# Six of 25 source-alpha lookups of a GAT layer as gathers from a table in DRAM, with residual steps moved

## Chip, cores, metric

One core of one Trainium2 chip runs the whole kernel. The metric is device time in microseconds of one launch, median of the runs shown.

## What is computed

Two graph attention layers over N = 3125 nodes and E = 53125 edges (sorted by destination, a self loop for each node in the list and one more added in each layer), on x of 3125 x 768, added to x:

```python
h = jnp.maximum(_layernorm(x), 0.0)
# one layer: xl = (h @ W).reshape(n, heads, out_ch)
alpha_src = jnp.einsum('nhc,hc->nh', xl, a_src)
alpha_dst = jnp.einsum('nhc,hc->nh', xl, a_dst)
e = jax.nn.leaky_relu(alpha_src[src] + alpha_dst[dst], 0.2)
m = jax.ops.segment_max(e, dst, num_segments=n)
e = jnp.exp(e - m[dst])
s = jax.ops.segment_sum(e, dst, num_segments=n)
alpha = e / (s[dst] + 1e-16)
out = jax.ops.segment_sum(xl[src] * alpha[:, :, None], dst, num_segments=n)
```

Layer 1 has 4 heads of 256 channels (joined to 1024), layer 2 one head of 768. After each layer come a layer norm and a residual product: layer 1 adds h @ Wr1 + br1 after a ReLU, layer 2 h1 @ Wr2 + br2. The change concerns `alpha_src[src]` of layer 1.

## The kernel before

The nodes are cut into NB = 25 tiles of 128 destinations (the last has 53). The edges of a tile stand in J = 17 slots of 128 each (fewer in the last), so one tile has 2176 slots. For each slot `idx_s` holds the source node, `rel_s` the destination within the tile.

The program runs in this order.

1. **Products.** For each tile x is normalised and multiplied by W1; eight more columns give the source and destination alphas of the 4 heads. The rows go to `table1` in DRAM (L218 stores them on SP), the alphas to `asad1` in SBUF (L876, ACT). Beside this the slot lists are made, and the destination alphas of all slots (`own`). 80 KB of one-hot per tile go to DRAM from POOL (L939).
2. **Residual tiles.** The residual h0 @ Wr1 of the twelve tiles kept in SBUF is a generator, `early()`: 24 residual tiles, each of six matmuls of 128 x 512 (L1008, f32, two records each in the profile), after which ACT adds the bias out of PSUM (L1011) and SP stores the result (L1015). It yields after every matmul: one yield is one step, 144 in all. The PSUM tile `pm` has three buffers. Steps are handed out between other work of TensorE (`next(fill, None)`).
3. **Lookups of source alphas** (loop at L1083). For each of the 25 tiles SP loads the list of source nodes modulo 128, 544 KB (L1087, tile `s`), DVE makes a one-hot of it (L530, `ohs`) and one of the source's tile number (L1090, `ohh`); TensorE multiplies the one-hot by all alphas, 51 matmuls into four PSUM tiles `pq` (L562); DVE picks the right tile's column (four L564) and reduces to `al1[:, :, :, b]` (L567). Ahead of each lookup stand 4 or 5 steps.
4. **Weights** (L1101, function `weights`). 17 transposes turn the alphas into rows (L581), DVE runs a maximum over each destination in both directions (L627, L628), 17 transposes turn it back (L592), DVE and ACT make the exponentials. The argument `(5, 13, 8)` gives the steps ahead of, between and behind the transposes.
5. **Sums of layer 1.** For each tile the rows of `table1` are gathered by POOL, 128 rows of 4 KB at a time, into 16 buffers (L197, L201), and TensorE adds them up by weight (L757), tile by tile in five rounds. `pace` gives for each tile and round how many steps of the late tiles' residual (`later()`, two matmuls per step, L182) stand behind the round. In the first rounds of the first tile `first()` also makes the totals: transposes (L581), a scan (L648), transposes back (L592).
6. **Layer 2**: products, gathers and sums of the second table, and the output.

The order on TensorE is the order of the code. In stages 2 and 3 ACT, DVE, POOL and SP are ordered by a scheduler from dependences and its own estimates; each engine then runs its list in that order, and an instruction that waits holds up those behind it.

Of the kernel before, what the change touches and what calls it, by code (L numbers as in the profile page):

```python
# [10 lines left out]
F32 = mybir.dt.float32  # L11
# [5 lines left out]
AF = mybir.ActivationFunctionType  # L17
# [13 lines left out]
J = 17  # L31
# [7 lines left out]
POS = [FROM[j % 4] + j // 4 for j in range(J)]  # L39
# [29 lines left out]
def in_order(  # L69
# [16 lines left out]
    nc = tc.nc  # L86
    N, D = x.shape
    E = src.shape[0]
    H, C1 = a_src1.shape
    HC = H * C1  # L90
    C2 = W2.shape[1]
    P = 128
    NB = -(-N // P)
# [32 lines left out]
    dram = ctx.enter_context(tc.tile_pool(name="dram", bufs=1, space=DRAM))  # L126
# [9 lines left out]
    src16_d = dram.tile([NB * S], I16, name="src16_d")  # L136
    slo16_d = dram.tile([NB * S], I16, name="slo16_d")
    keep_d = dram.tile([H * NB, S + 2], BF16, name="keep_d")
    hot_d = dram.tile([NB, 128, WIN], F8, name="hot_d")
    ball_d = dram.tile([C2], F32, name="ball_d")  # L140

# [17 lines left out]
    idx_s = const.tile([128, NB * J], I32, name="idx_s")  # L159
# [10 lines left out]
    asad1 = const.tile([P, NB, 2 * H], F32, name="asad1")  # L170
# [45 lines left out]
    def store_rows(q, dst_, b, t):  # L216
        for o, e in pieces(b):
            q.dma_start(dst_[b * P + o:b * P + e, :], t[o:e])  # L218
# [379 lines left out]
    def weights(heads, own, al, alo, keep, sr, xs, pp, nq, fill, steps):  # L598

        R = heads * NB  # L600

        def fl(t):
            return t.rearrange("p j h b -> p (j h b)")

        def leaky(t):
            nc.vector.scalar_tensor_tensor(fl(t), fl(t), SLOPE, fl(t), op0=OP.mult, op1=OP.max)  # L606

        def filled(n):
            for _ in range(n):
                next(fill, None)  # L610

        eo = sr.tile([128, J, heads, NB], F32, name="eo")
        m = sr.tile([128, J, heads, NB], F32, name="m")
        pen = sr.tile([R, S + 2], BF16, name="pen")
        fw = sr.tile([R, S], F32, name="fw")
        bw = sr.tile([R, S], F32, name="bw")
        nc.vector.tensor_scalar(pen, keep, -1.0, BIG, op0=OP.add, op1=OP.mult)
        a_s, a_d = own[:, :, :heads, :], own[:, :, heads:, :]
        to_rows, to_slots = rows_and_slots(heads, pp, "pq", nq)

        filled(steps[0])
        for _ in to_rows(al, xs):
            pass
        filled(steps[1])
        nc.vector.tensor_add(eo, a_s, a_d)
        leaky(eo)
        nc.vector.tensor_tensor_scan(fw, pen[:, 0:S], xs, 0.0, op0=OP.add, op1=OP.max)  # L627
        nc.vector.tensor_tensor_scan(bw[:, ::-1], pen[:, 1:S + 1][:, ::-1], fw[:, ::-1], 0.0,  # L628
                                     op0=OP.add, op1=OP.max)
        nc.vector.tensor_add(al, al, a_d)  # L630
        leaky(al)
        for _ in to_slots(bw, lambda js, p: nc.vector.tensor_max(m[:, js], p, a_s[:, js])):
            pass
        filled(steps[2])
        nc.vector.tensor_add(m, m, a_d)
        leaky(m)
        nc.vector.tensor_sub(al, al, m)
        nc.scalar.activation(al, al, AF.Exp)
        nc.vector.tensor_sub(eo, eo, m)
        nc.scalar.activation(alo[:, :, :heads, :], eo, AF.Exp)  # L640
# [133 lines left out]
    with tc.tile_pool(name="m1", bufs=1) as mp:  # L774
# [8 lines left out]
        with tc.tile_pool(name="h0", bufs=1) as hp, tc.tile_pool(name="pm1", bufs=1, space=PSUM) as pm1, \  # L783
# [9 lines left out]
            with tc.tile_pool(name="w1", bufs=1) as wp, tc.tile_pool(name="d1", bufs=2) as dp, \  # L793
# [60 lines left out]
                def product(b, i):  # L854

                    nonlocal known
                    r = rows_of(b)
                    if i == 0:
                        rows1[b] = wp.tile([P, HC], F32, name="row", bufs=LEAD)[:r]
                    row = rows1[b]  # L860
                    pm = pm1.tile([128, 512], F32, name="pm", bufs=3)
                    parts = 1 if r == P else 2
                    n = C // parts
                    for k in range(NK1):
                        for h in range(parts):
                            o = i * C + h * n
                            dense(pm[:, :n], h0[b][:, k, :], w1[:, k, o:o + n], r,
                                  start=(k == 0), stop=(k == NK1 - 1), at=half_at(b, h).start)
                        if k == NK1 - 1:
                            for h in range(parts):  # L870
                                o = i * C + h * n
                                e = min(o + n, HC) - o
                                at = half_at(b, h)
                                nc.scalar.activation(row[:, o:o + e], pm[at, :e], AF.Copy)
                                if e < n:
                                    nc.scalar.activation(asad1[:r, b, :], pm[at, e:n], AF.Copy)  # L876
                            if i == 2:
                                known = b + 1
                                store_rows(nc.sync, table1, b, row)
                        if k % 3 == 2:  # L880
                            yield
# [148 lines left out]
            with tc.tile_pool(name="pq1", bufs=1, space=PSUM) as pp:  # L1030
                with tc.tile_pool(name="sb1", bufs=1) as sb:
# [3 lines left out]
                    def ends_of_lists():  # L1035
# [40 lines left out]
                        yield  # L1076
                        yield from last_slots(sb, upto)

                    nc.sync.dma_start(keep1, keep_d)
                    by_chunk(g1, None, NK2, g1_c)  # L1080
                    by_chunk(be1, None, NK2, be1_c)
                    slots = ends_of_lists()
                    for b in range(NB):  # L1083
                        for _ in range(4 + b % 2):
                            next(fill, None)
                        t = sb.tile([128, S], I16, name="s", bufs=2)
                        nc.sync.dma_start(t, slo16_d[b * S:(b + 1) * S][None, :].to_broadcast([128, S]))  # L1087
                        ohs = one_hot(sb, t, S, "ohs")
                        ohh = sb.tile([128, J, NB], BF16, name="ohh", bufs=3)
                        nc.vector.tensor_tensor(  # L1090
                            ohh, iota_f[:, None, :NB].to_broadcast([128, J, NB]),
                            hi_s[:, b * J:(b + 1) * J, None].to_broadcast([128, J, NB]), OP.is_equal)
                        source_values(H, al1, b, pp, 4, group_of(H), ohs, tabs, ohh, pick)
                        next(slots, None)
                    for _ in slots:
                        pass
                    none = sb.tile([128, NB * J], F32, name="none")
                    nc.vector.tensor_scalar(none, rel_s, 0.0, float(CODE), op0=OP.is_lt, op1=OP.mult)
                    nc.vector.tensor_tensor(idx_k, none, idx_s, OP.add)
                with tc.tile_pool(name="sr1", bufs=1) as sr:  # L1100
                    weights(H, own, al1, alo1, keep1, sr, xs1, pp, 4, fill, (5, 13, 8))  # L1101
                for _ in fill:
                    pass

# [1 line left out]
        with tc.tile_pool(name="w2", bufs=1, reuse_waits="tile") as wp, tc.tile_pool(name="e1", bufs=2, reuse_waits="tile") as ep, \  # L1106
# [53 lines left out]
            def end1(b, z, share):  # L1160
# [50 lines left out]
                for i, (pm, (o, n)) in enumerate(zip(pms, halves)):  # L1211
# [4 lines left out]
                store_rows(nc.sync, table2, b, row)  # L1216

            places = [*range(2, 13), 0, 1, 13, 14, 15]
            pace = [(0, 0, 4, 5, 5), (4, 4, 3, 2, 2), (2.2, 3.4, 0, 0, 1), (3, 0, 0, 0.5, 3), (0, 0, 0.8, 3.4, 0),
                    (0, 0.8, 2.2, 3.4, 0)]  # L1220
            sums(H, C1, table1, al1, alo1_d, places, 3, gp, ap, pp, end1, more, pace, first())

# [756 lines left out]
```

## Time and profile before

| | |
|---|---|
| time, median of 3 runs | 1751.04 us (1750.64 to 1751.28) |
| profiled execution | 1749.32 us, span 1747.4 us |
| TensorE busy | 1635.8 us, 94% of the span |
| DVE / POOL / ACT busy | 1000.0 / 883.6 / 461.4 us |
| chain that ended last | TensorE 68%, DMA 18%, DVE 5% |
| granted TensorE clock, mean | 0.979 |

PE is TensorE's matmuls, PEld its weight loads, DVE VectorE, ACT ScalarE, POOL GpSimd, SP the engine that issues most plain DMAs. A timeline row gives start, duration, engine, line, operation, output and inputs, the count of records merged, and in brackets the idle time ahead of it and what ended that. A group's row gives busy time, mean ns of one, idle time ahead and its releasers. Matmuls of one row overlap a little, so a piece of work is best priced from start to start.

### The profile page before, as it was taken

The numbers are of one execution on the slowest core, as the hardware profiler recorded it, in microseconds if no ns is written. First come the engines' busy times: TensorE is split into PE (matmuls) and PEld (weight loads), VectorE is DVE, ScalarE is ACT, GpSimd is POOL, SyncE is SP. The second block draws the span as 40 slices with busy tenths as digits, with TensorE's granted clock in tenths as the row PEclk, the third lists the DMA queues.
The fourth block names the chain that finished last, engine by engine and source line by source line (L and its number), as shares of the span: only waits on it lengthen the run. The fifth ranks groups of instructions, "written<-read, shape, count | busy, mean of one in ns | idle before, by whom it ended". The sixth has DMA issues, their size and how long they took to land.

```text
span 1747.4 us, 31393 instructions
## 1 busy us (share of the span) xinstructions
PE 1635.8 (94%) x11519; PEld 929.9 (53%) x11519; DVE 1000.0 (57%) x2592; ACT 461.4 (26%) x1312; POOL 883.6 (51%) x924
## 2 busy tenths in 40 slices
PE   7999999899989999999999999987898999998994
PEld 5666666566646556556565555543444444444431
DVE  7783342798884666565565656751344544454555
ACT  2122332000122122122122121122344443434443
POOL 2000111200055766666666666736677777777773
PEclk9999999999999999999999999998999999999997
DMA  7824545743179999999999999979999999999994
GB/s 239 276 98 137 153 123 171 277 129 115 50 273 381 405 398 398 373 399 379 393 392 373 370 374 372 399 276 329 377 381 384 387 390 383 376 372 392 381 357 161
DMA packets 189924, 541.31 MB, mean 310 GB/s; under 512 B 34824, under 2 KB 83336, under 8 KB 189634
## 3 DMA queue, kind: packets, MB, share of 16 engines
q0 software_dynamic: 100912, 381.56, 57.6%
q1 hardware_dynamic: 84456, 147.27, 24.3%
q10 hardware_dynamic: 4394, 10.39, 1.5%
q8 instruction: 94, 1.54, 0.4%
q14 instruction: 68, 0.56, 0.1%
HBM read 498.62 MB, written 65.62 MB: 323 GB/s over the span
## 4 chain that ended last, share of the span: by engine, by line
PE 68%; DMA 18%; DVE 5%; issue 3%; POOL 3%; ACT 2%; POOLq 0%; SPq 0%; DVEq 0%; ACTq 0%
PE p L182 13%; DMA g<-table,idx_s 13%; PE pr L182 13%; PE pm L182 12%; PE pa L757 11%; PE pm L1008 7%; PE pa L1406 4%; PE pq L562 3%; DMA g<-table,hi_s 3%; POOL g L197 2%; PE mix L1365 1%; PE p L1182 1%; DMA w<-in_L_gnn_W_dram 1%; DMA s<-slo_d 1%; PE pt L840 1%
## 5 line engine op out<-in xcount | busy, mean ns | idle before, releaser
L197 POOL DMA_INDIRECT g<-table,idx_s x409 | 392.4, 959 | 334.9 <-DVE al L606 170.5
L201 POOL DMA_INDIRECT g<-table,hi_s x423 | 431.9, 1021 | 205.9 <-PE pa L757 88.8
L182 PE MATMUL pr<-wr,h 128*128 128x384 f32 x768 | 277.0, 507 | 3.3 <-issue 2.1
L182 PE MATMUL p<-w,h1T 128*128 128x384 f32 (+1 forms) x768 | 267.7, 496 | 0.0
L757 PE MATMUL pa<-g,w 128*32 128x256 f32 x3912 | 245.0, 384 | 9.4 <-DMA g<-table,hi_s 4.7
L182 PEld LDWEIGHTS pr<-wr,h 128*128 128x128 f32 x768 | 143.0, 196 | 112.7 <-issue 36.5
L182 PEld LDWEIGHTS p<-w,h1T 128*128 128x128 f32 x768 | 139.9, 189 | 112.9 <-issue 21.4
L757 PEld LDWEIGHTS pa<-g,w 128*32 128x32 f32 x3912 | 119.6, 110 | 128.5 <-issue 23.6
L1406 PE MATMUL pa<-g,w 128*32 128x384 f32 x1956 | 182.9, 504 | 2.6 <-DVE v L1440 2.6
L734 DVE TENSOR_TENSOR w<-oh,al 128x128 f32<-128x128 f32 (+1 forms) x416 | 132.3, 318 | 51.6 <-PE pa L757 26.8
L182 PE MATMUL pr<-h0k,wr 128*128 128x256 f32 (+1 forms) x576 | 142.2, 394 | 0.1
L1008 PE MATMUL pm<-h0g,wr 128*128 128x512 f32 x288 | 132.0, 606 | 0.0
L182 PE MATMUL pm<-w,h0l 128*128 128x344 f32 x432 | 131.9, 460 | 0.0
L182 PE MATMUL pm<-w,h0g 128*128 128x344 f32 x432 | 130.8, 459 | 0.3 <-ACT h0g L842 0.3
L939 POOL DMA_DIRECT2D hot_d<-ohd x25 | 13.4, 537 | 216.1 <-DVE own L513 122.0
L182 PEld LDWEIGHTS pr<-h0k,wr 128*128 128x128 f32 x576 | 106.5, 191 | 29.6 <-issue 10.3
L1406 PEld LDWEIGHTS pa<-g,w 128*32 128x32 f32 x1956 | 55.7, 112 | 118.1 <-issue 100.8
L733 DVE TENSOR_SCALAR oh<-iota_f,rel_s 128x32 f32<-128x32 f32 (+1 forms) x416 | 112.0, 269 | 2.0 <-issue 1.9
L182 PEld LDWEIGHTS pm<-w,h0g 128*128 128x128 f32 x432 | 81.9, 193 | 40.6 <-issue 1.6
L182 PEld LDWEIGHTS pm<-w,h0l 128*128 128x128 f32 x432 | 81.2, 192 | 39.3 <-issue 1.6
L1347 ACT ACTIVATE slots<-g 128x32 f32<-128x32 f32 x416 | 65.7, 219 | 121.2 <-DMA g<-table,idx_s 113.8
L1215 DVE COPY asad<-p 128x2 f32<-128x2 f32 (+1 forms) x25 | 4.0, 160 | 154.3 <-ACT row L1213 154.3
(302 smaller groups left out, 1702.5 us busy)
## 6 DMA issues: line engine op xcount, KB each, us to landing
s<-slo_d SPq DMA_DIRECT2D x25, 544.0 KB
table<-row SPq DMA_DIRECT2D x24, 512.0 KB
own<-table SPq DMA_DIRECT2D x24, 512.0 KB
h1T_d<-h1T SPq DMA_DIRECT2D x24, 512.0 KB
h<-h1T_d SPq DMA_DIRECT2D x88, 128.0 KB
table<-row SPq DMA_DIRECT2D x24, 392.0 KB
ring<-in_x_dram SPq DMA_DIRECT2D x24, 384.0 KB
out_dram<-z ACTq DMA_DIRECT2D x24, 384.0 KB
```

What stands on the lines that cost most here:

```text
L182: nc.tensor.matmul(out_, lhsT, rhs, start=start, stop=stop)
L197: nc.gpsimd.indirect_dma_start(out=g, out_offset=None, in_=table[:, :], in_offset=bass.IndirectOffsetOnAxis(ap=idx_s[:, c], axis=0))
L201: nc.gpsimd.indirect_dma_start(out=g, out_offset=None, in_=table[:, :], in_offset=bass.IndirectOffsetOnAxis(ap=idx_k[:, c], axis=0), bound ...
L562: nc.tensor.matmul(q[:, j], oh[:P, o:o + 128], tabs[:, i], start=(i == 0), stop=(i == 2))
L733: nc.vector.tensor_scalar(oh, iota_f[:, lo:hi], rel_s[:, c:c + 1], None, op0=OP.is_equal)
L734: nc.vector.tensor_tensor(w, oh[:, None, :].to_broadcast([128, heads, hi - lo]), al[:, POS[j], :, b:b + 1].to_broadcast([128, heads, hi - ...
L757: nc.tensor.matmul(pa[p0:p0 + 32, o // f, o % f:o % f + n], w[:, o // cols, :], g[:, o:o + n], start=to not in opened, stop=False, skip_gr ...
L840: nc.tensor.transpose(pt[:, k, :r], xt[:, (k0 + k) * 128:(k0 + k + 1) * 128], ident[:r, :r])
L1008: nc.tensor.matmul(pm, wr1[:, k, m * 128:(m + 1) * 128], groups[gi][:, k, :], start=(k == 0), stop=(k == NK1 - 1))
L1182: nc.tensor.transpose(pt[:, k, :r], z[:, (k0 + k) * 128:(k0 + k + 1) * 128], ident[:r, :r])
L1347: nc.scalar.activation(slots[b % 2][:, POS[j], :], gs[b, j][:, C2:C2 + 1].to_broadcast([128, 32]), AF.Copy)
L1406: nc.tensor.matmul(pa[p0:p0 + 32, i, :f], w_, g[:, i * f:(i + 1) * f], start=(i, q) not in opened, stop=False, skip_group_check=True)
```

## The change

The alphas of each tile are also stored as rows of a table `asrc_d` (3125 x 4 floats) in DRAM, 25 small DMAs on SP. Tiles 18 to 23 are no longer looked up: POOL gathers their alphas from that table, 17 gathers per tile of 128 rows of 16 bytes, and after the loop ACT copies each tile's result into `al1`. The other 19 tiles are looked up as before, with 102 steps spread over them and five more ahead of the first. The third argument of `weights` goes from 8 to 13, and `pace` of the first tile moves steps from its later rounds to its second.

```diff
+    asrc_d = dram.tile([N, H], F32, name="asrc_d")
...
                             if i == 2:
                                 known = b + 1
+                                nc.sync.dma_start(asrc_d[b * P:b * P + r], asad1[:r, b, :H])
                                 store_rows(nc.sync, table1, b, row)
...
+                    BY_GATHER, BESIDE = 6, 102
...
-                    for b in range(NB):
-                        for _ in range(4 + b % 2):
+                    by_gather = range(NB - 1 - BY_GATHER, NB - 1)
+                    read = {}
+                    for b in by_gather:
+                        read[b] = sb.tile([128, J, H], F32, name=f"read{b}")
+                        for j in range(J):
+                            c = b * J + j
+                            nc.gpsimd.indirect_dma_start(
+                                out=read[b][:, POS[j]], out_offset=None, in_=asrc_d[:, :],
+                                in_offset=bass.IndirectOffsetOnAxis(ap=idx_s[:, c:c + 1], axis=0))
+                    by_table = [b for b in range(NB) if b not in by_gather]
+                    for i, b in enumerate(by_table):
+                        for _ in range((i + 1) * BESIDE // len(by_table) - i * BESIDE // len(by_table) + (0 if i else 5)):
                             next(fill, None)
...
                     for _ in slots:
                         pass
+                    for b in by_gather:
+                        nc.scalar.activation(al1[:, :, :, b], read[b], AF.Copy)
...
-                    weights(H, own, al1, alo1, keep1, sr, xs1, pp, 4, fill, (5, 13, 8))
+                    weights(H, own, al1, alo1, keep1, sr, xs1, pp, 4, fill, (5, 13, 13))
...
-            pace = [(0, 0, 4, 5, 5), (4, 4, 3, 2, 2), (2.2, 3.4, 0, 0, 1), (3, 0, 0, 0.5, 3), (0, 0, 0.8, 3.4, 0),
+            pace = [(0, 3, 3, 4, 4), (4, 4, 3, 2, 2), (2.2, 3.4, 0, 0, 1), (3, 0, 0, 0.5, 3), (0, 0, 0.8, 3.4, 0),
```

How it moves instructions is shown at three places. Lines of the changed kernel are one to fifteen higher than before: L1011 becomes L1013, L197 L198, L757 L758.

ACT, from the last product on, before (`rt<-pm` is the activation behind a residual tile, `junk,cnt` a count over a one-hot, `scr<-pq` the copies behind the first 17 transposes of the weights):

```order
L876 ACTIVATE asad_108<-pm 53x8
L1011 ACTIVATE rt<-pm,br_c 128x4x128
L942 ACTIVATE junk,cnt<-ohd 128x640
L1011 ACTIVATE rt<-pm,br_c 128x4x128 x19
L583 ACTIVATE scr<-pq 100x512 x4
```

And at the same place in the changed kernel, where `al_117<-read` is the copy of one gathered tile:

```order
L1013 ACTIVATE rt<-pm,br_c 128x4x128
L1111 ACTIVATE al_117<-read_2366 128x68
L1013 ACTIVATE rt<-pm,br_c 128x4x128
L1111 ACTIVATE al_117<-read_2384 128x68
L1013 ACTIVATE rt<-pm,br_c 128x4x128
L1111 ACTIVATE al_117<-read_2402 128x68
L1013 ACTIVATE rt<-pm,br_c 128x4x128
L1111 ACTIVATE al_117<-read_2420 128x68
L1013 ACTIVATE rt<-pm,br_c 128x4x128
L1111 ACTIVATE al_117<-read_2438 128x68
L1013 ACTIVATE rt<-pm,br_c 128x4x128
L1111 ACTIVATE al_117<-read_2456 128x68
```

The first row there is the second residual activation; the six copies stand one ahead of each of the third to the eighth, not behind the loop as in the code.

POOL, behind the stores of one-hots, before (`g` is a buffer of the sums' gathers):

```order
L368 DMA w_in<-views_d,view 100x704
L939 DMA hot_d<-ohd 128x640 x25
L197 DMA g_4418<-table_64,idx_s 128x1024
L197 DMA g_4419<-table_64,idx_s 128x1024
L197 DMA g_4420<-table_64,idx_s 128x1024
```

And in the changed kernel:

```order
L941 DMA hot_d<-ohd 128x640 x25
L1092 DMA read_2366<-asrc_d,idx_s 128x4 x17
L1092 DMA read_2384<-asrc_d,idx_s 128x4 x17
L1092 DMA read_2402<-asrc_d,idx_s 128x4 x17
L1092 DMA read_2420<-asrc_d,idx_s 128x4 x17
L1092 DMA read_2438<-asrc_d,idx_s 128x4 x17
L1092 DMA read_2456<-asrc_d,idx_s 128x4 x17
L198 DMA g_4162<-table_64,idx_s 128x1024
```

All 102 small gathers go ahead of the first 4 KB gather.

TensorE, behind the last lookup, before (`pm` are residual steps, `pq<-ident` transposes, `pa` the first sum):

```order
L1008 MATMUL pm<-h0g_1348,wr_2272 128x512 x5
L581 MATMUL pq<-ident,al_116 100x128 x17
L1008 MATMUL pm<-h0g_1348,wr_2272 128x512 x13
L592 MATMUL pq<-ident,bw 128x100 x17
L1008 MATMUL pm<-h0g_1348,wr_2272 128x512 x8
L757 MATMUL pa<-g_4418,w_4435 32x256
```

And in the changed kernel:

```order
L1010 MATMUL pm<-h0g_1364,wr_2298 128x512 x5
L582 MATMUL pq<-ident,al_117 100x128 x17
L1010 MATMUL pm<-h0g_1364,wr_2298 128x512 x13
L593 MATMUL pq<-ident,bw 128x100 x17
L1010 MATMUL pm<-h0g_1364,wr_2298 128x512 x13
L758 MATMUL pa<-g_4162,w_4179 32x256
```

Five more steps stand ahead of the first sum. Two rounds of sums later, before (the transposes of the totals, then the third round):

```order
L581 MATMUL p_4536<-ident,al_116 100x128 x4
L581 MATMUL p_4542<-ident,al_116 100x128 x4
L581 MATMUL p_4548<-ident,al_116 100x128
L757 MATMUL pa<-g_4426,w_4522 32x256 x2
L757 MATMUL pa<-g_4427,w_4527 32x256
```

And in the changed kernel (`pr<-h0k` are the matmuls of the late tiles' residual):

```order
L582 MATMUL p_4280<-ident,al_117 100x128 x4
L582 MATMUL p_4286<-ident,al_117 100x128 x4
L582 MATMUL p_4292<-ident,al_117 100x128
L183 MATMUL pr<-h0k,wr_2298 128x256 x6
L758 MATMUL pa<-g_4170,w_4266 32x256 x2
```

Three steps (six matmuls), which stood in later rounds, now stand behind the totals' transposes.

## Prediction

> **What bounds the kernel now.** I read the page first, then the busy time by stage, then the timelines of PE, ACT, POOL and DVE in the stretch that the change rewrites. Three rows of the windows answer give that stretch; the columns are the window, its length, busy time of PE, PEld, DVE, ACT and POOL, then the granted clock, DMA share and GB/s.
>
> ```profile
> PE 1635.8 (94%) x11519; PEld 929.9 (53%) x11519; DVE 1000.0 (57%) x2592; ACT 461.4 (26%) x1312; POOL 883.6 (51%) x924
> 304.66:472.60 167.94, 162.91 (x1528) 102.92 (x1527) 140.48 (x226) 14.46 (x22) 10.87 (x11) 0.99 0.43 148
> 472.60:499.70 27.10, 22.14 (x79) 11.13 (x77) 26.45 (x17) 8.27 (x12) 7.58 (x5) 1.00 0.34 106
> 499.70:566.00 66.30, 60.60 (x524) 41.19 (x524) 33.32 (x107) 14.25 (x36) 38.78 (x35) 0.95 1.00 382
> ```
>
> PE sets the end nearly everywhere. In the lookup stage (304.66 to 472.60) it is busy 162.91 of 167.94 us, while POOL works 10.87. So whatever leaves PE there is a gain, unless PE is made to wait. PE's timeline prices both kinds of its work:
>
> ```profile
> 456.22 4.52 PE L1008 MATMUL pm<-h0g,wr 128*128 128x512 f32 x10
> 460.58 2.45 PE L562 MATMUL pq<-tabs,ohs 128*128 128x100 bf16 x51
> 462.86 3.66 PE L1008 MATMUL pm<-h0g,wr 128*128 128x512 f32 x8
> 466.36 2.45 PE L562 MATMUL pq<-tabs,ohs 128*128 128x100 bf16 x51
> 468.65 4.52 PE L1008 MATMUL pm<-h0g,wr 128*128 128x512 f32 x10
> 473.00 2.02 PE L581 MATMUL pq<-ident,al 128*100 128x128 f32 x17
> 474.86 11.32 PE L1008 MATMUL pm<-h0g,wr 128*128 128x512 f32 x26
> 487.11 1.65 PE L592 MATMUL pq<-ident,bw 100*128 100x100 f32 x17 [0.93 <-issue]
> 488.60 7.06 PE L1008 MATMUL pm<-h0g,wr 128*128 128x512 f32 x16
> 499.69 4.71 PE L757 MATMUL pa<-g,w 128*32 128x256 f32 x32 [4.04 <-DVE w L734]
> ```
>
> From start to start, one lookup takes 2.28 us (460.58 to 462.86) and a residual step (two L1008 records) 0.873 us (462.86 to 466.36 is four). After the lookups come the 17 transposes at 473.00, 13 steps, 17 transposes, 8 steps and a wait of 4.04 us before the sums begin at 499.69.
>
> **The change, part by part.** *Lookups removed.* Six times 2.28 is 13.7 us off PE, and five steps (4.4 us) move into the 4.04 us wait. If nothing waited, the 112 steps left after the first six, and 19 lookups, would follow from 306.48 on:
>
> ```profile
> 306.48 3.67 PE L1008 MATMUL pm<-h0g,wr 128*128 128x512 f32 x8
> 329.21 0.19 PE L1052 MATMUL pq<-mine_f,cnt 128*25 128x4 f32 x2 [4.35 <-DVE scr L564]
> 329.33 6.26 PE L1008 MATMUL pm<-h0g,wr 128*128 128x512 f32 x10
> ```
>
> 306.48 + 112 x 0.873 + 19 x 2.28 + 0.5 (three small matmul pairs) = 448.1, against 473.00 now: 24.9 us less. The early wait of 4.35 us (DVE was late) goes too in that count.
>
> *Gathers added.* 102 gathers of 16-byte rows stand first on POOL, ahead of the 4 KB gathers for the sums. None of that size is in the trace, so these rows bound it:
>
> ```profile
> L197 POOL DMA_INDIRECT g<-table,idx_s x409 | 392.4, 959 | 334.9 <-DVE al L606 170.5
> L699 POOL DMA_INDIRECT ao<-alo_d,at_last x25 | 24.7, 987 | 16.5 <-DMA alo_d<-scr 9.2 <-DVE aw L687 1.8 <-DVE oh L733 1.8
> 304.66 1.01 POOL L197 DMA_INDIRECT g<-table,idx_s  x1 [2.68 <-PE pm L1008]
> 308.49 1.21 POOL L197 DMA_INDIRECT g<-table,idx_s  x1 [0.30 <-issue]
> 313.87 0.94 POOL L197 DMA_INDIRECT g<-table,idx_s  x1 [0.30 <-issue]
> 317.60 0.98 POOL L197 DMA_INDIRECT g<-table,idx_s  x1 [0.30 <-issue]
> ```
>
> POOL's time per gather does not follow the bytes: 959 ns with rows of 3 to 4 KB, 987 with 800-byte rows (L699). What is common to them is 128 rows, as here. With the 0.30 us between them a gather costs 1.26 us; the ends are 1.24 (0.94 + 0.30) and 1.29 (304.66 to 317.60, ten gathers). So 17 gathers, one tile, take 21.4 us, and all six tiles 128.5. Begun at 304.9 (304.66 plus one more small store ahead on SP), the last leaves POOL at 433.1.
>
> *The copies added, and what queues behind them.* This decides. A tile's copy into al1 (L1111 of the changed kernel) waits for its 17 gathers and stands on ACT between the activations that empty PE's residual tiles (L1011, now L1013): the n-th copy ahead of activation n+2, as the order shows. A residual tile pm is six steps, and has three buffers, so tile n+5 cannot start on PE before activation n+2. PE runs in its written order; when it stops there, the lookups behind it stop as well.
>
> ```profile
> L1011 ACT ACTIVATE rt<-pm,br_c 128x512 f32<-128x512 f32 x24 | 16.5, 687 | 174.0 <-PE pm L1008 165.3 <-DMA s<-slo_d 6.9 <-issue 1.8
> L876 ACT ACTIVATE asad<-pm 128x8 f32<-128x8 f32 (+1 forms) x25 | 4.3, 172 | 0.0
> 124.60 0.97 SPq L410 DMA_DIRECT2D tails<-w_in  x1
> 126.89 0.35 DVE L412 SCALAR_TENSOR_TENSOR w_in<-tails,later,w_in 100x128 int32<-100x128 int32 x1 [0.41 <-DMA tails<-w_in]
> 309.56 8.09 DMA s<-slo_d
> ```
>
> From POOL's end to PE's restart I take 2.8 us: landing 1.7, between 1.3 (the DMA at 124.60 ends its record at 125.57, DVE has its data at 126.89) and 8.1 (the s load of 544 KB under eleven 4 KB gathers), nearer the small one; then the copy 0.2 (L876), the activation 0.69, hand-over 0.2. The Trainium skill, DMA: Bandwidth & Descriptors, section on the anatomy of a GpSimd DMA, gives about 2.0 us fixed per DMA; by that estimate the restart is 0.3 us later; no small gather stands in this trace to test it.
>
> Copy n therefore frees PE at 304.9 + 21.42n - 0.3 + 2.8: 328.8, 350.2, 371.7, 393.1, 414.5 and 435.9. PE comes to the six gates (after 30, 36, 42, 48, 54 and 60 steps) unhindered at 334.8, 342.3 and so on; for the last 306.48 + 54 x 0.873 + 9 x 2.28 + 0.5 = 374.6. The first gate is open. Then PE does 7.5 to 9.8 us of work between gates that are 21.4 apart: five waits, 8 to 14 us each, 61.3 in all (435.9 - 374.6).
>
> After 435.9 PE has 58 steps and ten lookups left: 50.6 + 22.8. The clock costs more: after the wait of 4.35 us the five steps at 329.33 took 6.26 us against 4.52 at 456.22, so 1.7 us (ends 0 and 1.7). And the loads of s for lookups 12 to 14 stand on SP behind stores of the eighth residual tile, so they start at about 438, under the 4 KB gathers; DVE has slack for most of it: 1 us (0 to 4). The transposes begin at 512.0, which is +39.0 against 473.00.
>
> *Steps moved into the wait before the sums.* 488.60 + 13 x 0.873 = 499.95 against 499.69: +0.3, and the wait is gone. Its five steps were counted out of the loop above.
>
> *Pace.* Three steps of the sums' residual (six matmuls, twelve records) move up behind the 9 transposes, ahead of the scan wait:
>
> ```profile
> 513.94 1.77 PE L592 MATMUL p<-ident,scr 100*128 100x100 f32 x10 [3.17 <-DVE scr L648]
> 515.51 4.66 PE L182 MATMUL pr<-h0k,wr 128*128 128x256 f32 x16
> ```
>
> Twelve records at 0.29 fill the 3.17. The first sum, 4.71 us on a cold clock behind DVE's w, may take 2 less. But DMA's share there is 1.00 (window row), so only part stays: -2.5, between 0 and -5.7 (all of PE's idle time, 66.30 - 60.60).
>
> *25 small stores of alphas* on SP, beside those of the table: nobody waits but the first gather; 0, at most +2 if loads behind them come late.
>
> Sum: +39.0 + 0.3 - 2.5 = **+36.8 us**. The profiled execution took 1749.32 us (1.9 outside its span of 1747.4), the median of the three runs is 1751.04; so 1786 by the one and 1788 by the other, and I predict 1788. 0.2% (3.5 us) is about what a measurement of this kernel can tell from no change.
>
> **The rivals.** *A. ACT's copies cost nothing, and the gathers are hidden as they were meant to be.* Then PE gains 24.9, loses 0.3, gains 2.5: 1751.0 - 27.1 = 1724. For it: 128.5 us of gathers do fit in the 143 us that PE then has. Against it: the copies are not at the end of ACT's order. It needs 17 gathers within 7.5 us, 0.44 each, or an ACT that overtakes. The point at which the change costs nothing is a last restart at 399.1: 0.90 us per gather, below the 1.24 of the shortest rows. The Trainium skill (TensorE: Matmul & The Clock Gate, section on the array's sub-arrays) calls ScalarE's queue strictly first-in first-out, which would exclude overtaking; no record of before shows ACT blocked with ready work behind it. 0.05.
>
> *B. DVE holds POOL up.* One case is plain:
>
> ```profile
> 509.19 4.69 DVE L648 TENSOR_TENSOR_SCAN scr<-keep,scr 100x2176 f32<-100x2176 bf16 x1 [4.55 <-ACT scr L583]
> 509.37 5.31 POOL L201 DMA_INDIRECT g<-table,hi_s  x1 [0.31 <-issue]
> L564 DVE TENSOR_TENSOR scr<-pq,ohh 128x500 f32<-128x500 f32 x100 | 56.7, 597 | 19.6 <-PE pq L562 19.6
> L567 DVE TENSOR_REDUCE al<-scr 128x68 f32<-128x1700 f32 x25 | 48.0, 1920 | 0.1
> L530 DVE TENSOR_SCALAR ohs<-s,node_f 128x2176 bf16<-128x2176 int16 x25 | 19.5, 778 | 6.3 <-DMA s<-slo_d 6.2
> L1090 DVE TENSOR_TENSOR ohh<-iota_f,hi_s 128x425 bf16<-128x425 f32 x25 | 14.9, 596 | 1.6 <-DMA table<-row 1.6
> ```
>
> The gather at 509.37 ends 0.8 us after the scan. DVE does four L564 and one of the others per lookup, 5.7 us, and nine lookups lie beside the gathers. If all of it stopped POOL the last restart came 51 us later: 1839; if half, 1813. Against it: the ten gathers at 304.66 lost 0.05 each to such work, which is in the 1.29. The Trainium skill, SBUF — State Buffer, section on its two sides, has the lock only for operations in a two-port mode or with two SBUF inputs, so L530 and L1090: 1.37 us per lookup, at most 12 in all, 1800 by that estimate; the 0.94 us rows fit it, since L564 reads PSUM. 0.08 above my range.
>
> *C. The residual buffers bind less than I say,* and waits end earlier, but not as early as in A: 1724 to 1778. 0.05, a third of it below 1747.5.
>
> **How the numbers follow.** The forecast has 0.82. Its bounds: gather 1.24 or 1.29 (-2, +3), landing (-0.4, +6.4), sums (-3.2, +2.5), clock and s loads (-2.7, +3), stores (+2). Downwards that is -8.3 in all, and with a little of C 1778; upwards +16.9, of which I take 14, since not all of it comes at once: 1802. Left out are A, C and the upper part of B, 0.18. Faster by over 0.2%: A and the third of C, 0.07. Within: 0.02. Slower: 0.91.
>
> **What would show it.** Right: POOL's gathers at 1.24 to 1.29 us; ACT's copies idle until DMA of read, 21 us apart; PE idle before L1010 five times, with ACT rt named; the 17 transposes near 512; the sums some 37 us later and then as before. Wrong: copies that wait under 2 us, gathers under 0.9 us, or transposes before 473.

## The result and the profile after

The changed kernel takes 1802.11 us, median of four executions (1799.35 to 1811.10); the kernel before took 1750.84 on the same chip (1749.50 to 1751.28, four). The ratio is 1.0303 with a 95% interval of 1.0266 to 1.0340: slower by 51.3 us, where +36.8 were forecast. The profiled execution took 1799.35 us, span 1797.5, so 50.1 more than the span before.

For the experiments below one thing must be known: e1 to e4 ran where the kernel before takes 1751 us, as here (the first condition); e5 to e18 ran later in another, in which the kernel before itself takes 1916 to 1930 us (the other condition), and are compared only with it and with each other there.

Windows of the changed kernel, cut at the first gather, PE's last restart, the transposes, the first sum and the transposes behind the scan (columns as in the prediction):

```profile
308.92:442.58 133.66, 78.84 (x574) 46.43 (x573) 55.26 (x114) 6.13 (x16) 101.98 (x105) 0.80 0.25 61
442.58:520.53 77.95, 75.93 (x626) 45.62 (x627) 54.17 (x70) 7.29 (x11) 8.33 (x9) 0.97 0.47 171
520.53:548.40 27.87, 26.02 (x88) 12.92 (x86) 27.47 (x23) 10.08 (x13) 7.57 (x5) 1.00 0.40 133
548.40:572.27 23.87, 17.08 (x126) 9.86 (x126) 12.46 (x33) 3.07 (x7) 7.98 (x8) 0.67 0.96 346
```

While POOL gathers, PE works 78.84 of 133.66 us, where it worked 162.91 of 167.94 in the lookup stage before; and it is idle for another 6.8 us in the 23.87 behind the first sum. The groups of the three new kinds of work, and ACT's timeline around the first and the last two copies:

```profile
L1010 PE MATMUL pm<-h0g,wr 128*128 128x512 f32 x288 | 139.0, 632 | 55.3 <-ACT rt L1013 54.8 <-DMA wr<-in_L_gnn_Wr_dram 0.4
L1092 POOL DMA_INDIRECT read<-asrc_d,idx_s x102 | 100.0, 980 | 36.5 <-issue 30.8 <-PE pd L546 5.7
L1111 ACT ACTIVATE al<-read 128x68 f32<-128x68 f32 x6 | 2.0, 327 | 122.3 <-DMA read<-asrc_d,idx_s 122.3
```

```profile
333.90 0.33 ACT L1111 ACTIVATE al<-read 128x68 f32<-128x68 f32 x1 [19.10 <-DMA read<-asrc_d,idx_s]
334.07 0.67 ACT L1013 ACTIVATE rt<-pm,br_c 128x512 f32<-128x512 f32 x1
...
420.67 0.33 ACT L1111 ACTIVATE al<-read 128x68 f32<-128x68 f32 x1 [21.12 <-DMA read<-asrc_d,idx_s]
421.19 0.69 ACT L1013 ACTIVATE rt<-pm,br_c 128x512 f32<-128x512 f32 x1 [0.20 <-ACT al L1111]
441.70 0.33 ACT L1111 ACTIVATE al<-read 128x68 f32<-128x68 f32 x1 [19.82 <-DMA read<-asrc_d,idx_s]
441.86 1.25 ACT L1013 ACTIVATE rt<-pm,br_c 128x512 f32<-128x512 f32 x2
```

ACT stands idle for 19 to 21 us ahead of each copy; the activation that PE needs starts 0.16 to 0.24 us after the copy's start, once (at 421.19) 0.52. PE's side, and its way from the last gate to the first sums:

```profile
355.89 2.08 PE L1010 MATMUL pm<-h0g,wr 128*128 128x512 f32 x2 [11.54 <-ACT rt L1013]
378.17 2.08 PE L1010 MATMUL pm<-h0g,wr 128*128 128x512 f32 x2 [11.35 <-ACT rt L1013]
399.59 6.25 PE L1010 MATMUL pm<-h0g,wr 128*128 128x512 f32 x10 [8.63 <-ACT rt L1013]
421.93 7.03 PE L1010 MATMUL pm<-h0g,wr 128*128 128x512 f32 x10 [12.87 <-ACT rt L1013]
442.58 6.08 PE L1010 MATMUL pm<-h0g,wr 128*128 128x512 f32 x8 [10.42 <-ACT rt L1013]
458.18 2.44 PE L563 MATMUL pq<-tabs,ohs 128*128 128x100 bf16 x51 [2.02 <-DVE scr L565]
520.53 2.02 PE L582 MATMUL pq<-ident,al 128*100 128x128 f32 x17
548.40 2.24 PE L758 MATMUL pa<-g,w 128*32 128x256 f32 x32 [0.93 <-ACT rt L1013]
557.84 2.23 PE L582 MATMUL p<-ident,al 128*100 128x128 f32 x9 [4.32 <-ACT scr L584]
559.86 2.77 PE L183 MATMUL pr<-h0k,wr 128*128 128x256 f32 x6
563.49 1.22 PE L183 MATMUL pr<-h0k,wr 128*128 128x256 f32 x2 [0.86 <-DMA h0k<-h0T_d]
567.54 1.22 PE L183 MATMUL pr<-h0k,wr 128*128 128x256 f32 x2 [0.79 <-DMA h0k<-h0T_d]
572.27 1.75 PE L593 MATMUL p<-ident,scr 100*128 100x100 f32 x10
```

Five waits for ACT's rt, 54.8 us in all. Then comes a second loss that the prediction does not have: a wait of 4.32 us for ACT's scr, and three steps that take from 559.86 to 568.69, since the pieces of h0k land 2 us apart. ACT and SP beside it, and in the last row ACT at the same place in the kernel before:

```profile
547.91 9.18 ACTq L1130 DMA_DIRECT2D h0k<-h0T_d  x5
548.37 2.19 SPq L1017 DMA_DIRECT2D r1T_d<-rt  x4
550.61 0.52 SPq L215 DMA_DIRECT2D own<-table  x1
555.70 8.08 SPq L1130 DMA_DIRECT2D h0k<-h0T_d  x5
557.19 1.08 ACT L584 ACTIVATE scr<-p 100x512 f32<-100x512 f32 x2 [8.84 <-DMA own<-table]
```
```profile
499.81 4.54 ACTq L1115 DMA_DIRECT2D h0k<-h0T_d  x4
```

ACT needs 9.18 us to issue five loads of h0k, and what ends its idle time is SP's load of `own`: in the program each of these issues waits on a completion counter that an earlier DMA of SP uses too, the last one on that of this load. The load stands on SP behind the stores of the last moved residual tile, which start at 548.37. ACT's copies out of PSUM (L584) stand behind the issue. In the kernel before the last four issues took 4.54 us; their counters were those of stores, none that of `own`.

Where each profiled execution is (us from its start; the last three rows relative to before for the changed kernel are +58.3, +56.0, +50.1):

| | before | changed | e1 | e2 | e3 | e4 |
|---|---|---|---|---|---|---|
| 17 transposes | 473.00 | 520.53 | 450.07 | 450.70 | 470.94 | 469.16 |
| first sum | 499.69 | 548.40 | 478.96 | 478.58 | 498.81 | 495.85 |
| transposes behind the scan | 513.94 | 572.27 | 504.07 | 502.44 | 522.94 | 510.81 |
| last sum of layer 1 | 1163.4 | 1219.4 | 1150.4 | 1146.9 | 1169.2 | 1160.6 |
| end | 1747.4 | 1797.5 | 1733.7 | 1729.9 | 1754.1 | 1743.6 |

From the last sum to the end the changed kernel's profiled execution took 578.1 us, all the others 583.0 to 584.9, and it is the fastest of its four. So I take these 5 to 7 us as a chance of this one execution; no run shows a cause.

### The profile page after: what moved, and what is told of

It is laid out like the page before. It is cut to its first block, busy times and chain, and to the rows that moved or that the text cites. A ratio compares the mean times of both kernels' runs of the same rounds, so it can differ in the third digit from the quotient of the medians.

```text
span 1797.5 us, 30902 instructions
## 1 busy us (share of the span) xinstructions
PE 1632.5 (91%) x11213; PEld 920.5 (51%) x11213; DVE 969.4 (54%) x2550; ACT 461.6 (26%) x1318; POOL 979.7 (55%) x1026
## 4 chain that ended last, share of the span: by engine, by line
PE 54%; DMA 21%; DVE 9%; POOL 8%; issue 5%; ACT 2%; SPq 1%; POOLq 0%; DVEq 0%; ACTq 0%
PE pr L183 13%; PE p L183 12%; DMA g<-table,idx_s 12%; PE pa L758 11%; PE pm L183 7%; POOL read L1092 6%; DMA g<-table,hi_s 4%; PE pa L1421 4%; PE pm L1010 2%; POOL g L198 1%; DMA w2k<-in_L_gnn_W_dram 1%; PE pq L563 1%; PE p L1197 1%; PE mix L1380 1%; DMA w<-in_L_gnn_W_dram 1%
## 5 line engine op out<-in xcount | busy, mean ns | idle before, releaser
L198 POOL DMA_INDIRECT g<-table,idx_s x409 | 391.2, 956 | 242.8 <-PE pq L593 83.2
L758 PE MATMUL pa<-g,w 128*32 128x256 f32 x3912 | 246.1, 388 | 6.1 <-DMA g<-table,hi_s 2.6
L1010 PE MATMUL pm<-h0g,wr 128*128 128x512 f32 x288 | 139.0, 632 | 55.3 <-ACT rt L1013 54.8
L758 PEld LDWEIGHTS pa<-g,w 128*32 128x32 f32 x3912 | 119.4, 111 | 126.1 <-issue 24.8
L735 DVE TENSOR_TENSOR w<-oh,al 128x128 f32<-128x128 f32 (+1 forms) x416 | 132.1, 318 | 56.4 <-PE pa L758 31.4
L1092 POOL DMA_INDIRECT read<-asrc_d,idx_s x102 | 100.0, 980 | 36.5 <-issue 30.8
L1010 PEld LDWEIGHTS pm<-h0g,wr 128*128 128x128 f32 x288 | 55.4, 201 | 119.5 <-issue 58.5
```

The costliest lines, as they stand in the source:

```text
L198: nc.gpsimd.indirect_dma_start(out=g, out_offset=None, in_=table[:, :], in_offset=bass.IndirectOffsetOnAxis(ap=idx_s[:, c], axis=0))
L735: nc.vector.tensor_tensor(w, oh[:, None, :].to_broadcast([128, heads, hi - lo]), al[:, POS[j], :, b:b + 1].to_broadcast([128, heads, hi - ...
L758: nc.tensor.matmul(pa[p0:p0 + 32, o // f, o % f:o % f + n], w[:, o // cols, :], g[:, o:o + n], start=to not in opened, stop=False, skip_gr ...
L1010: nc.tensor.matmul(pm, wr1[:, k, m * 128:(m + 1) * 128], groups[gi][:, k, :], start=(k == 0), stop=(k == NK1 - 1))
L1092: nc.gpsimd.indirect_dma_start(out=read[b][:, POS[j]], out_offset=None, in_=asrc_d[:, :], in_offset=bass.IndirectOffsetOnAxis(ap=idx_s[:, ...
```

## Experiments

**Theory 1:** ACT's copies, ahead of the activations that free PE's residual tiles, hold PE. **Theory 2:** the moved steps lose at the beginning of the sums instead of gaining. **Rivals:** the gathers themselves cost the time by contention; the terms of the prediction for the moved steps.

### e1 and e2: the copies elsewhere

```diff
-                        nc.scalar.activation(al1[:, :, :, b], read[b], AF.Copy)
+                        nc.gpsimd.tensor_copy(al1[:, :, :, b], read[b])   # e1
```
```diff
+                    with tc.manual_schedule(engines={ACT}):               # e2, around the loop and the copies
                     for i, b in enumerate(by_table):
```

> The six copies stand on POOL, behind the 102 gathers, so ACT waits for no gather; PE's and DVE's orders are those of the changed kernel. Theory 1 (ACT's copies, ahead of the activations that free PE's residual tiles, hold PE at the last five gates): no wait of PE for ACT's rt in the lookup stage, the 17 transposes at about 449.5 (448.1 by start-to-start prices plus the 1.2 us by which the product stage ends later) against 520.53 in the changed kernel; the last gather still ends near 439.7. Theory 2 (the step moved into the wait ahead of the sums delays ACT's own h0k issues and with them the first sums by about 10 us) holds beside it, so the whole is 1749.3 - 23.5 + 9.6 = about 1735, 1727 to 1738 if some of it is made up later. Rival (the gathers themselves, by contention with DVE, the loads of s or PE, cost the 47 us): about 1800 still. Rival A of the prediction, with no loss at the sums: 1724.

> The six copies stay on ACT, but ACT keeps the written order in the lookup stage, so that they come behind the 19 residual activations. Theory 1: the same as with the copies on POOL, within 3 us (1727 to 1738), because the place in the queue decides and not the engine. Rival (ACT is too slow or blocked for another reason): above 1780. Contention rival: about 1800.

e1 took 1735.04 us (1728.07 to 1739.26, six), e2 1731.91 (1730.98 to 1740.41, six), before 1751.22 (23 executions): ratios 0.9900 (0.9876 to 0.9924) and 0.9901 (0.9878 to 0.9925). e2: ACT, PE and POOL:

```profile
440.56 1.31 ACT L1112 ACTIVATE al<-read 128x68 f32<-128x68 f32 x5
442.88 0.34 ACT L1112 ACTIVATE al<-read 128x68 f32<-128x68 f32 x1 [1.02 <-DMA read<-asrc_d,idx_s]
```
```profile
450.70 2.02 PE L582 MATMUL pq<-ident,al 128*100 128x128 f32 x17
478.58 2.24 PE L758 MATMUL pa<-g,w 128*32 128x256 f32 x32 [0.93 <-ACT rt L1013]
488.24 1.85 PE L582 MATMUL p<-ident,al 128*100 128x128 f32 x9 [4.54 <-ACT scr L584]
493.70 0.70 PE L183 MATMUL pr<-h0k,wr 128*128 128x256 f32 x2 [1.26 <-DMA h0k<-h0T_d]
```
```profile
439.89 0.95 POOL L1092 DMA_INDIRECT read<-asrc_d,idx_s  x1 [0.30 <-issue]
461.23 6.12 POOL L198 DMA_INDIRECT g<-table,idx_s  x1 [0.30 <-issue]
```

The last gather leaves POOL as late as in the changed kernel (439.89 against 438.71), but the transposes are at 450.70, 22.3 ahead of before. Only the copies' place differs (PE, DVE, POOL and SP have the same order in both programs): it is worth 0.0402 of 1751, 70 us. That it is the same on POOL shows that the place in a queue decides, not the engine. The rest of theory 2 is there too: of the 22.3 us only 11.5 are left at the transposes behind the scan. In this condition both versions beat both kernels, the kernel before by 1.0%.

### e3: the moved steps alone

```diff
-                        for _ in range(4 + b % 2):
+                        for _ in range((b + 1) * 107 // NB - b * 107 // NB):
-                    weights(H, own, al1, alo1, keep1, sr, xs1, pp, 4, fill, (5, 13, 8))
+                    weights(H, own, al1, alo1, keep1, sr, xs1, pp, 4, fill, (5, 13, 13))
-            pace = [(0, 0, 4, 5, 5), (4, 4, 3, 2, 2), ...
+            pace = [(0, 3, 3, 4, 4), (4, 4, 3, 2, 2), ...
```

> The kernel before, 25 lookups and no gathers, with only the residual steps moved: 107 steps beside the lookups, 13 in the wait ahead of the sums, three more of the sums' residual behind the first transposes. Theory 2: the wait of 4.04 us goes and the sums begin at about 495.5, but the second load of own stands behind the moved step's stores, ACT's h0k issue waits for it, and the scan starts about 9.6 later in relation to that: layer 1 ends at +3 (0 to +6) and the time is 1749 to 1757. The prediction's own terms (-4.1 for the wait and -2.5 for the pace) give 1744.5.

1754.77 us (twelve), ratio 1.0021 (1.0004 to 1.0037): 0.7 to 6.5 us slower, as theory 2 had it and not the prediction's terms. e3, PE and ACT behind the first sum:

```profile
498.81 2.33 PE L757 MATMUL pa<-g,w 128*32 128x256 f32 x32 [0.93 <-ACT rt L1011]
502.08 1.93 PE L757 MATMUL pa<-g,w 128*32 128x256 f32 x32
507.72 2.23 PE L581 MATMUL p<-ident,al 128*100 128x128 f32 x9 [3.70 <-ACT scr L583]
512.12 1.22 PE L182 MATMUL pr<-h0k,wr 128*128 128x256 f32 x2 [0.46 <-DMA h0k<-h0T_d]
518.22 1.22 PE L182 MATMUL pr<-h0k,wr 128*128 128x256 f32 x2 [0.80 <-DMA h0k<-h0T_d]
522.94 1.15 PE L592 MATMUL p<-ident,scr 100*128 100x100 f32 x10
```
```profile
498.32 8.64 ACTq L1115 DMA_DIRECT2D h0k<-h0T_d  x5
507.07 1.08 ACT L583 ACTIVATE scr<-p 100x512 f32<-100x512 f32 x2 [8.31 <-DMA own<-table]
```

The wait of 4.04 us is gone and the first sum 0.9 earlier (I had expected 495.5, 4.2 earlier), but the transposes behind the scan are 9.0 later. No small gather stands in this kernel, so the loss is the moved steps' own.

### e4: the gathers, with nothing reading them

```diff
+                    for b in range(NB - 7, NB - 1):      # ahead of the 25 lookups, which all stay
+                        read = sb.tile([128, J, H], F32, name=f"read{b}")
+                        for j in range(J):
+                            c = b * J + j
+                            nc.gpsimd.indirect_dma_start(
+                                out=read[:, POS[j]], out_offset=None, in_=asrc_d[:, :], ...
```

The 25 stores into `asrc_d` are in it too; the copies are not, and the lookups are those of before.

> The kernel before with all 25 lookups, with the 25 stores of alphas and the 102 gathers added; nothing reads what they fetch, and there are no copies. Theory 1: PE is not held, POOL's 102 gathers run 1.285 us apart and end near 440; the time is that of before plus 0 to 3 us (the product stage ends 1.2 later). Contention rival: the lookups' PE or DVE work takes longer by a third or more of the 47 us, 1765 or above.

1748.79 us (twelve), ratio 0.9992 (0.9978 to 1.0005): no difference. One window of e4, POOL working at the gathers:

```profile
300.00:440.00 140.00, 138.43 (x1310) 86.94 (x1298) 120.45 (x211) 12.39 (x21) 102.05 (x103) 1.00 0.49 145
```

PE works 138.43 of 140 us beside 102 gathers. So contention explains none of the 51 us here.

### e5 to e14 and e17: the parts of the moved steps, and fewer gathers

All with ACT in the written order (e2) but e8 and e12, which are the changed kernel with three tiles by gather:

```diff
-                    weights(..., fill, (5, 13, 13))     # e5, e9, e13: all three back; e7, e11, e14, e17: these two back
-                    BY_GATHER, BESIDE = 6, 102
+                    weights(..., fill, (5, 13, 8))
+                    BY_GATHER, BESIDE = 6, 107
-            pace = [(0, 3, 3, 4, 4), ...                # e6, e10: this one back
+            pace = [(0, 0, 4, 5, 5), ...
```
```diff
-                    BY_GATHER, BESIDE = 6, 102          # e8, e12
+                    BY_GATHER, BESIDE = 3, 102
```

> Copies late on ACT, and the residual steps where they were before the change (five more beside the lookups, 8 ahead of the sums, the old pace). Transposes at about 454.5, first sum at about 481.3 (26.7 later, as in the kernel before), 2.7 later than with the late copies alone; but PE's wait for ACT's scr ahead of the last nine transposes (4.54 us) and the three for h0k (3.4 us) are gone. Theory 2: the last sum of layer 1 at about 1145 against 1146.9, the time 1727 to 1733, no slower than 1731.9. The prediction's terms (moved steps gain 6.6): about 1738.

> Copies late, 13 steps ahead of the sums, the old pace. Theory 2 in its parts: ACT's h0k issue still waits for the second load of own, so PE still waits 3 to 5 us for ACT's scr; but no step of the sums' residual stands ahead of the scan, so the waits for h0k and the slow first steps (9.6 us for three steps) go; the time is 1726 to 1733. If the pace is not to blame: as with the late copies alone, 1731.9, with scan and second transposes at the same place.

> Copies late, 8 steps ahead of the sums as before, the new pace. Theory 2 in its parts: the h0k issue on ACT waits only for stores of residual rows, so PE's wait for ACT's scr is under 1 us and those for h0k under 1 us together; the gain of the moved pace then stays, 1725 to 1731. If the pace alone is to blame: waits for h0k of 2 us or more and 1732 or above.

> The changed kernel with three tiles by gather instead of six, 22 lookups, the copies on ACT where the scheduler puts them, ahead of activations 3 to 5. Theory 1 by its own arithmetic: the third copy frees PE at 378.2; 76 steps (66.3) and 16 lookups (36.5) and the cold clock (1.7) follow, so the transposes are at 483 to 485 against 473.00, and with 3 us at the sums the time is 1765 (1760 to 1769). Contention rival, in proportion to the gathers: half of 51, 1776.

> The kernel of e5, to be measured where the kernel before takes about 1751 us. First sum at about 481.3, no wait for ACT's scr or for h0k above 1 us at the sums' beginning, the last sum of layer 1 at about 1145. Theory 2: 1727 to 1733; the prediction's terms (moved steps gain 6.6): about 1738. If PE's gaps between single matmuls (2.56 us, named issue) on the other chip belong to the small gathers as such, they show here too and the time is above 1800.

> The kernel of e6 under the same condition: 13 steps ahead of the sums, old pace. Theory 2 in its parts: 3 to 5 us of wait for ACT's scr (it waits behind the h0k issue for own), no wait for h0k ahead of the scan; 1726 to 1733.

> The kernel of e7 under the same condition: 8 steps ahead of the sums, new pace. Theory 2 in its parts: waits for ACT's scr and for h0k under 1 us each, the gain of the moved pace stays; 1725 to 1731. If the pace alone is to blame: waits for h0k of 2 us or more, 1732 or above.

> The kernel of e8 under the same condition: three tiles by gather, copies early on ACT. Theory 1: the third copy frees PE at 378.2, transposes at 483 to 485, 1765 (1760 to 1769). Contention in proportion to the gathers: 1776.

> Copies late on ACT, the residual steps where they were before the change. Where the kernel before takes about 1751: theory 2 has 1727 to 1733, the prediction's terms about 1738. Where it takes about 1927: 2047 again.

> Copies late, 8 steps ahead of the sums as before, the new pace. Where the kernel before takes about 1751: theory 2 in its parts 1725 to 1731, waits for ACT's scr and for h0k under 1 us each; if the pace alone is to blame 1732 or above. Where it takes about 1927: 2046 again.

> Copies late, 8 steps ahead of the sums as before, the new pace. Where the kernel before takes about 1751: theory 2 in its parts 1725 to 1731, waits for ACT's scr and for h0k under 1 us each; if the pace alone is to blame 1732 or above. Where it takes about 1927: 2046 again.

All met the other condition. Totals: with copies late 2035.5 to 2049.7 us, ratios 1.059 to 1.062 to the kernel before there (all intervals within 1.0564 and 1.0648), and no difference between the variants; three tiles 1995.38 and 1996.53 (1.0335 and 1.0360; 1.0306 to 1.0389 by both intervals). One execution of e5 took 5861 us and one of e7 4557; the ratios leave them out. Every total expected for the first condition (1725 to 1776) is so far off, and the arithmetic of e8 (1765) is left without a test. The numbers that e13, e14 and e17 give for the other condition repeat what had been measured before them (2047, 2046, 2046); they came out at 2046.83, 2044.83 and 2035.52. Why this condition is slower is in the next section.

What they can speak to is the part played by each half of the moved steps, at a place where the small gathers are long done. From the transposes of bw to those behind the scan (L593 to L593, L592 in the kernel before; single executions), and in the last two rows the same stretch in the first condition:

| | us |
|---|---|
| neither moved: e5, e9, e13, e15, e18 | 29.2, 29.2, 29.2, 29.2, 29.1 |
| five steps ahead of the sums: e6, e10 | 30.9, 30.1 |
| new pace: e7, e11, e14, e17 | 31.4, 30.8, 34.6, 36.7 |
| both: e16, e8, e12 | 37.0, 38.0, 38.4 |
| first condition, neither: before, e4 | 26.8, 27.5 |
| first condition, both: changed, e1, e2, e3 | 37.6, 39.9, 37.6, 37.9 |

The five steps cost 1 to 2 us, the pace 1.6 to 7.5, both together 8 to 9 (10 to 13 in the first condition). PE ahead of the transposes behind the scan, three rows of e17, and one of e11, the same kernel; in both ACT is not held by `own`:

```profile
631.63 1.91 PE L183 MATMUL pr<-h0k,wr 128*128 128x256 f32 x4
634.44 1.22 PE L183 MATMUL pr<-h0k,wr 128*128 128x256 f32 x2 [0.89 <-DMA h0k<-h0T_d]
640.52 1.22 PE L183 MATMUL pr<-h0k,wr 128*128 128x256 f32 x2 [0.80 <-DMA h0k<-h0T_d]
```
```profile
636.57 0.70 PE L183 MATMUL pr<-h0k,wr 128*128 128x256 f32 x2 [0.41 <-DMA h0k<-h0T_d]
```

In e17 the pieces of h0k land 2.0 us apart beside the 4 KB gathers and PE waits 3.3 us for them in all, though ACT issued them early; e14 waits 2.4, e7 0.9 and e11 0.4. So my expectation for the pace alone (waits for h0k under 1 us) failed in two of four executions of one kernel, and how late this load lands is not fixed by the program. With the five steps alone (e6, e10) the expected wait of 3 to 5 us behind ACT came, 4.5 and 3.7 us, but the stretch got only 1 to 2 us longer by it. Both halves are thus seen to cost something, a load that isn't there yet and a queue behind `own`; neither alone comes reliably to what both cost, and which is the larger stays open. So does what each is worth in the end: the totals there differ by less than their spread.

### e15, e16, e18: what the gathers do in the other condition

> The kernel before with 25 stores and 102 small gathers that nothing reads. Where the kernel before takes about 1751: within 3 us of it, as e4. Where it takes about 1927: if the small gathers alone slow PE's instruction stream, PE shows gaps of 2.5 us named issue from 310 to 440 and the time is 2040 to 2070; if it is the copies or the shorter lookup stage, it stays within 10 us of before.

> The changed kernel itself. Where the kernel before takes about 1751: 1802 again. Where it takes about 1927: PE is held by the copies until 443 in any case, and the gaps of the instruction stream lie inside these waits; so the lookups left at 443 are those that the slow stream did not get done, 2040 to 2070 as with late copies, and the place of the copies no longer matters.

> The kernel before itself. Where it takes about 1751: the profile as it was. Where it takes about 1927: if gathers of any size starve PE, it shows gaps named issue from 304 to 318 and all through the sums; if only those of small rows do, none in the lookup stage and none in the sums of layer 1, whose gathers have 4 KB rows, and the 177 us lie elsewhere.

e15, the kernel of e4, took 2068.00 us, ratio 1.0706 (1.0682 to 1.0731); e16, the changed kernel, 2049.29, 1.0613 (1.0593 to 1.0634). e18, the kernel before, took 1906.58 in one execution. The window of e15 that was shown of e4, and PE in it:

```profile
300.00:440.00 140.00, 39.79 (x261) 19.09 (x253) 19.66 (x47) 4.60 (x12) 99.39 (x104) 0.60 0.20 48
```
```profile
360.00 0.24 PE L563 MATMUL pq<-tabs,ohs 128*128 128x100 bf16 x1 [2.56 <-issue]
362.80 0.24 PE L563 MATMUL pq<-tabs,ohs 128*128 128x100 bf16 x1 [2.56 <-issue]
```

The same kernel, the same gathers at the same 0.945 us in the median, but PE starts one matmul in 2.80 us and waits for nothing that the profile names, from 323 on (at first in shorter gaps) until 469, 16 us after POOL's last gather of that stretch. Its transposes are at 613.78 against 475.05 in e18, +138.7, as much as the medians differ (2068.00 and 1930.19); the two profiled executions, on two chips, end 162.7 apart, and the other 24 us I can't place. Both totals, 2068 and 2049, lie in the 2040 to 2070 that I expected for this condition. In e16 and with late copies PE is so far behind at 440 that the copies' place no longer matters (transposes at 593.2 in e16 as in e9). In the kernel before POOL is quiet in the lookup stage but for eleven gathers, and beside those PE has two such gaps of 1.1 us; e18's last sum of layer 1 is at 1194.5 (+31.1 to the first profile), and from there it takes 710.2 us where it took 584.0. The sums of layer 2 in e18, and below them as first profiled:

```profile
L1406 PE MATMUL pa<-g,w 128*32 128x384 f32 x1956 | 231.0, 525 | 73.3 <-issue 66.8 <-DVE v L1440 6.5
```
```profile
L1406 PE MATMUL pa<-g,w 128*32 128x384 f32 x1956 | 182.9, 504 | 2.6 <-DVE v L1440 2.6
```

There too PE waits for nothing named (issue, 66.8 us) while POOL gathers; in the sums of layer 1 such waits come to 12.4 us. It is not a property of one chip: e17 and e18 ran on the chip of e1 to e4. Single instructions a fixed 2.80 us apart look like an instruction stream that arrives late. But from 330 to 384 of e15 the profile has 28 matmuls of PE and no packet in the DMA queues that load instructions, so these matmuls did not each wait for such a load. No row shows what they wait for; that stays open, and with it why gathers of 16-byte rows do it more than those of 3 to 4 KB.

## Why the prediction was wrong, step by step

Right in direction and in the main mechanism, and short by 14.5 us: 1802.11 lies 0.11 above its range. The step that failed is what the moved steps do at the beginning of the sums (below). That the total is so near is in part luck: at the transposes behind the scan the forecast is 21.5 us short in the profiled execution, of which 2.3 are made up within layer 1 and 5.9 behind it by something that no run explains.

- *Copies queue ahead of the residual activations, five gates.* Held, by e1 and e2: without it the transposes come at 450.70. Forecast waits 8 to 14 us each, 61.3 in all; measured 8.63 to 12.87, 54.8. The Trainium skill's strict first-in first-out order of ScalarE's queue (TensorE: Matmul & The Clock Gate, section on the array's sub-arrays) agrees with the rows: no L1013 passes a copy that waits, each starts 0.16 to 0.52 us after the copy's start. Rival C, waits that end earlier, did not come: PE's last restart is at 442.58 where 435.9 was forecast.
- *First gather at 304.9.* It came at 308.92: +4.0. Of this 1.2 is a product stage that ends later (last alphas copied at 301.65 against 300.44), the rest the time from that copy to the first gather: 7.3 us (7.2 in e1 and e2, 6.6 in e4), where it was 4.2 before and 5.0 in e3, which have no such stores. In the program the gather waits for the last stores to land; the profile names only PE's pd as what ended POOL's wait. "Nobody waits but the first gather" was true, and that gather was the head of the chain; 0 to +2 was too little.
- *1.26 us per gather.* 1.285 (0.980 + 0.30, 308.92 to 438.71 in 101): within its ends, +2.5 in all. Rival B, DVE holding POOL up, is at most 0.04 us per gather, some 4 us in all. Where it does show is e2's 4 KB gather at 461.23, 6.12 us beside DVE's scan, and nobody waits for that one.
- *2.8 us from POOL's end to PE's restart.* 439.65 to 442.58, 2.9; landing 2.05 (439.65 to 441.70; 1.7 to 2.3 over the six tiles) where I took 1.7. The Trainium skill's figure (DMA: Bandwidth & Descriptors, section on the anatomy of a GpSimd DMA, about 2.0 us fixed) was the better one.
- *76.1 us from restart to transposes.* 77.95: the wait for the late s was 2.02 instead of 1, the clock cost about 1 more. (A step is 0.875 us by the rows that the prediction quotes, not 0.873; it changes nothing.) These four terms make the transposes +47.5 instead of +39.0.
- *Weights +0.3, pace -2.5, cover for the moved steps.* This is the step that failed in kind, the largest part of the miss: from the first sum to the transposes behind the scan it took 9.6 us longer than before (23.87 against 14.25), where the pace was to gain 2.5. The moved steps do fill the wait of 4.04 (first sum 27.87 behind the transposes, as 26.69 + 0.3 + 0.9), but their stores were not followed past SP's load of `own`, nor that load into the counter on which ACT's issue of h0k waits; and the steps of the pace were costed at their PE time without a look at when h0k lands. At the transposes behind the scan +58.3 stands where +36.8 was forecast; 2.3 are made up by the last sum. e3 measures the moved steps at +3.6 us (0.7 to 6.5) on the whole, where my terms, with the five steps out of the loop, make -6.6.
- *Rival A, 1724, the copies at no cost.* As a statement on the changed kernel it was wrong; with the copies late the gathers are hidden, and e2's 1731.9 falls short of 1724 by 7.9 us, about the 10.2 by which e3 and my terms for the moved steps differ.
- *The end of the execution.* +56.0 at the last sum of layer 1 became +50.1 in the profiled execution; the three others took 1.3 to 11.8 us longer than it.

The signs that I named: gathers at 1.24 to 1.29, copies idle until the DMA of read and 21 to 22 us apart, five waits for ACT's rt are all there; transposes near 512 and sums 37 later "and then as before" are not.

## What to carry to other kernels

A result that arrives late should be fetched by an instruction that stands late in its engine's queue: six copies of 0.33 us cost 70 us by standing ahead of the activations that empty PE's buffers, and nothing behind them. A step moved into a wait brings along its stores and its loads: follow each through the queues and completion counters that it shares, and see when its data land, before counting its engine time as hidden. And a gather that is free beside PE in one run may not be in another (e4 and e15), so a gain built on it should be measured on more than one occasion.

## What the runs showed of the hardware

- 102 gathers of 128 rows of 16 bytes took PE nothing in e4 (138.43 us of work in 140) and some 99 us of that in e15 (39.79), the same program both times.
- A gather of 16-byte rows takes POOL 0.94 us at best and 0.98 in the mean (0.96 for those of 3 to 4 KB rows, L198), and its data are there 1.7 to 2.3 us behind POOL's end.
- A DMA issue can hold its engine for a DMA of another queue: five issues on ACT took 9.18 us (four took 4.54 before), the idle time behind them ended by a load that SP had issued.
